# End-node one-hots and the run mask: from one block after the last gathers to single pieces between the groups

## The chip, the cores and the metric

The kernel runs on one core of one Trainium2 chip. The time is device microseconds (us) of one execution. The engines are TensorE (PE, with its weight loads as PEld), VectorE (DVE), ScalarE (ACT), GpSimd (POOL, which here issues the gathers) and SyncE (SP, which issues most other transfers).

## The reference, cut to what matters

Two graph layers run over 12,500 nodes with 256 features and 200,000 edges. The edges come sorted by `dst`.

```python
h = relu(layernorm(x))
x = x + segment_sum(edge_weight * (h @ W)[dst], src)          # first layer
h = relu(layernorm(x))
q, k, v = h @ Wq.T + bq, h @ Wk.T + bk, h @ Wv.T + bv         # 8 heads of 32
sim = sum_d(q[dst] * k[src]) / sqrt(32)                       # per edge and head
p = exp(sim - segment_max(sim, dst)[dst])
attn = p / segment_sum(p, dst)[dst]
x = x + segment_sum(attn * v[src], dst) @ Wo.T + bo           # second layer
```

All is in float32.

## The kernel before, in words

The first layer (`layer0`) sorts the edges by `src` on the chip, gathers rows, sums them by matmuls, and writes the tables Q and KV that the second layer reads. In its course `prep_a`, `prep_c` and `prep_s` turn the edge lists into columns, once for each of four blocks `b` of up to 128 groups. `prep_c` leaves the source ids in `ci0` to `ci3`, and `prep_s` leaves negated places of the end nodes in `nsl0` to `nsl3`. Both are tiles of 128 partitions by 512 elements, in which a group has four columns. `prep_s` also writes to memory, for each group, its first and its last end node (table `PD`).

The second layer (`layer1`) takes the sorted edges in 391 groups of 512, each as four columns of 128 edges. One group passes these steps:

- `load_l1` (three steps ahead): SP loads the 80 rows of Q from the group's first end node on; POOL gathers the KV rows of the 512 edges by four indirect transfers (line 974) that read their ids from `ci`.
- `onehot_t` and `similarity`: ACT makes the transposed one-hots, PE spreads Q to the edges (line 1007), DVE multiplies with K (line 1008) and sums by head (line 1009).
- `softmax_steps`, for eight groups together: DVE scans the maxima of runs of equal end nodes (lines 1030 and 1034), ACT takes the exponential.
- 11 steps later (`LAG`): DVE weighs V (`weigh`, line 1073), ACT makes the one-hots from `nsl` (`onehot`, line 991), PE sums by end node (`aggregate`, line 1085), and the sums go to the table AG.
- Beside these, finished blocks of AG are divided, multiplied by Wo, added to x and stored (lines 836 to 883).

A gathered group lies in one of 15 buffers named `kvt`; a buffer comes free when `weigh` has read it.

An end node can span two or more groups. So the first and last end node of each group are kept apart: 2 x 391 = 782 partial rows (table `PR`), with their maxima in `pm`. `merge_steps` joins them after the groups. It splits the 782 into 7 blocks, one of 14 and six of 128. For each block `k` it needs `S[:, k]` (which rows of the block have the same end node), `C[:, k]` (which rows have the node of the last row of the block before), a count `cnt` of equal rows ahead (only the first of equal rows is stored, the others go to spare rows), the ids `nid` and `idx`, and the mask `mk` of runs for two scans over the 782 maxima.

The function `loads` (step 388 of the loop) brings `PD` in twice: spread over all partitions as `pdr` (line 1183) and as columns `pdc` (lines 1184 and 1185). The function `same` (step 389) then makes `nid`, `C`, `S`, `cnt`, `idx` and `mk` in one go, on DVE (lines 1196 to 1213). The large tiles of the merge are taken from the `kvt` buffers (`big`). Then come `load_rows` (390), `own_rows` (391, gathers of x on POOL, line 1246), `factors` (395, the scans and the exponential), and for each block `total`, `ends_norm`, `ends_turn`, `ends_mult`, `ends_add` and `ends_put`, until step 408.

In both layers the order of work on each engine is the order in which the code is written (a manual schedule). `layer1` runs its steps `t` in order, and a table `todo` hangs further functions at a place 0, 1 or 2 of a step: 0 is between `weigh` of group t - 11 and `similarity` of group t, 1 is after `similarity`, 2 is after `aggregate`. Each engine works its own queue in that order and waits for the others by semaphores.

Of the kernel before, what the change touches and what calls it, by code (L numbers as in the profile page):

```python
# [77 lines left out]
class Gnn:  # L78
# [90 lines left out]
    def prep_c(self, b):  # L169
        nc, cp, wp = self.nc, self.kp, self.wp  # L170
        ng = min(P, NG - b * P)
        si, di, ei = self.raw
        df = self.k0.tile([P, G], F32, name=f"df{b}")
        nc.vector.tensor_copy(df, di)
        self.df[b] = df
        gb = cp.tile([P, 7], F32, name=f"gb{b}")
        nc.vector.tensor_copy(gb[:, 1:2], df[:, 0:1])
        nc.vector.tensor_copy(gb[:, 2:3], df[:, G - 1:G])
        nc.vector.tensor_scalar(gb[:, 3:4], df[:, 0:1], 1.0, None, op0=ALU.add)
        for j, c, o in ((4, PACE * (1 + 1e-5), -OL - 1), (5, PACE * (1 - 1e-5), OU)):  # L180
            v = gb[:, j:j + 1]
            nc.vector.tensor_scalar(v, self.pcol, c, c * (b * P + o), op0=ALU.mult, op1=ALU.add)
            nc.vector.tensor_scalar(v, v, 0.0, None, op0=ALU.max)
            nc.vector.tensor_scalar(v, v, v, None, op0=ALU.mult)
        nc.vector.tensor_scalar(gb[:, 0:1], df[:, 0:1], gb[:, 4:5], float(N - P), op0=ALU.max, op1=ALU.min)
        nc.vector.tensor_scalar(gb[:, 6:7], df[:, 0:1], gb[:, 4:5], gb[:, 5:6], op0=ALU.max, op1=ALU.min)
        gi = cp.tile([P, 7], I32, name=f"gi{b}")
        nc.vector.tensor_copy(gi, gb)
        self.gb[b], self.gi[b] = gb, gi
        sf = wp.tile([P, G], F32, name="sf", bufs=1)  # L190
        nc.vector.tensor_copy(sf, si)
        ci = self.csi[b] = cp.tile([P, P, W], I32, name=f"ci{b}")
        if b < NPT:
            self.cols(sf, ng, [ci])
            return
        sh = wp.tile([P, G], I16, name="sh", bufs=1)
        nc.vector.tensor_copy(sh, si)
        nc.sync.dma_start(self.SR[:ng], sh[:ng])
        l0 = self.l0r = self.k0.tile([P, G], F32, name="l0r")
        nc.vector.tensor_scalar(l0, df, gb[:, 0:1], None, op0=ALU.subtract)  # L200
        self.csf, self.cl0, self.cew = [self.k0.tile([P, P, W], F32, name=f"c{k}") for k in range(3)]
        self.cols(sf, ng, [self.csf, ci])
        self.cols(l0, ng, [self.cl0])
        self.cols(ei, ng, [self.cew])
# [698 lines left out]
    def prep_s(self, b):  # L903
# [24 lines left out]
        nc.vector.tensor_tensor(t, t, sl, op=ALU.max)  # L928
        nc.vector.scalar_tensor_tensor(sl, sl, float(QW + 1), isl, op0=ALU.subtract, op1=ALU.mult)
        nc.vector.tensor_sub(sl, sl, t)  # L930
        self.nsl[b] = self.kp.tile([P, P, W], F32, name=f"nsl{b}")
        self.cols(sl, ng, [self.nsl[b]])
        mk = wp.tile([P, G + 4], F32, name="mk", bufs=1)
        nc.vector.tensor_tensor(t, pf, df, op=ALU.not_equal)
# [2 lines left out]
        nc.vector.memset(mk[:, G:], NEG)  # L937
        nc.sync.dma_start(self.MK[b * P:b * P + ng], mk[:ng])
        nc.sync.dma_start(self.PD[b * 2 * P:(b + 1) * 2 * P].rearrange("(p c) -> p c", c=2), gb[:, 1:3])
        nc.vector.tensor_tensor(t, pf, df, op=ALU.is_gt)  # L940
        nc.vector.tensor_tensor(bad, bad, t, op=ALU.max)
        late = wp.tile([P, 2], F32, name="late")
# [215 lines left out]
    def merge_steps(self):  # L1158
# [7 lines left out]
        def big(n, *shape):  # L1166
            t = wp.tile([P, W * 2 * D], F32, name="kvt", bufs=LAG + PRE + 1)[:, :n]
            if shape:
                t = t.rearrange("p (k d) -> p k d", k=shape[0])
            return t  # L1170

        def size(k):
            return P if k else R0

        def rows(k):
            return slice(R0 + (k - 1) * P, R0 + k * P) if k else slice(0, R0)

        def loads():
            b = big(2 * KB * P)
            pdr, S = b[:, :KB * P], b[:, KB * P:].rearrange("p (k e) -> p k e", k=KB)  # L1180
            pdc = wp.tile([P, KB], F32, name="pdc", bufs=1)
            nc.vector.memset(pdc, -1.0)
            nc.sync.dma_start(pdr, bass.AP(tensor=pd.tensor, offset=pd.offset, ap=[[0, P], [1, KB * P]]))
            nc.sync.dma_start(pdc[:R0, 0:1], pd[:R0][:, None])
            nc.sync.dma_start(pdc[:, 1:, None], bass.AP(tensor=pd.tensor, offset=pd.offset + R0,
                                                        ap=[[1, P], [P, KB - 1], [1, 1]]))
            T.update(pdr=pdr, S=S, pdc=pdc)

        def same():
            pdr, S, pdc = T["pdr"], T["S"], T["pdc"]  # L1190
            cnt = wp.tile([P, KB], F32, name="cntm", bufs=1)
            tr = wp.tile([P, KB], F32, name="trm", bufs=1)
            scr = wp.tile([P, P], F32, name="scrm", bufs=1)
            T["idx"] = wp.tile([P, KB], I32, name="idxm", bufs=1)
            T["nid"] = wp.tile([P, KB], I32, name="nidm", bufs=1)
            nc.vector.tensor_scalar(T["nid"], pdc, 0.0, None, op0=ALU.max)
            T["C"] = big(KB * P, KB)
            for k in range(KB):
                r, m = size(k), pdr[:, rows(k)]
                if k:  # L1200
                    nc.vector.tensor_scalar(T["C"][:, k], m, pdc[:, k - 1:k], self.ident[:, size(k - 1) - 1:size(k - 1)],
                                            op0=ALU.is_equal, op1=ALU.mult)
                nc.vector.tensor_scalar(S[:, k, :r], m, pdc[:, k:k + 1], None, op0=ALU.is_equal)
                nc.vector.scalar_tensor_tensor(scr[:, :r], S[:, k, :r], 1.0, self.lower[:, :r], op0=ALU.mult, op1=ALU.mult,
                                               accum_out=cnt[:, k:k + 1])
            nc.vector.tensor_scalar(tr, cnt, 0.0, self.trash, op0=ALU.is_gt, op1=ALU.mult)
            nc.vector.tensor_tensor(T["idx"], tr, pdc, op=ALU.max)
            b = big(2 * NR + 2)
            mk, f = b[:H, :NR + 1], b[:H, NR + 2:]
            nc.vector.memset(mk[:, 0:1], NEG)  # L1210
            nc.vector.memset(mk[:, NR:], NEG)
            nc.vector.tensor_tensor(mk[:, 1:NR], pdr[:H, 1:NR], pdr[:H, :NR - 1], op=ALU.not_equal)
            nc.vector.tensor_scalar(mk[:, 1:NR], mk[:, 1:NR], NEG, None, op0=ALU.mult)
            T.update(mk=mk, f=f)

        def load_rows():
# [33 lines left out]
        def space(n, w):  # L1250
            T[n] = big(KB * w, KB)

        def total(k):
            r, rt, fc = size(k), T["rt"], T["fc"]
            sc = wp.tile([P, D + H], F32, name="scm", bufs=2)
            nc.vector.tensor_tensor(sc[:r, :D].rearrange("p (h d) -> p h d", h=H),
                                    rt[:r, k, :D].rearrange("p (h d) -> p h d", h=H),
                                    fc[:r, k, :, None].to_broadcast([r, H, DH]), op=ALU.mult)
            nc.vector.tensor_mul(sc[:r, D:], rt[:r, k, D:], fc[:r, k])
            pg = tp.tile([P, G], F32, name="ps", bufs=1)[:, :D + H]  # L1260
            nc.tensor.matmul(pg[:r], T["S"][:r, k, :r], sc[:r], start=True, stop=(k == 0))
            if k:
                q = size(k - 1)
                nc.tensor.matmul(pg[:r], T["C"][:q, k, :r], T["ms"][:q, k - 1], start=False, stop=True)
            nc.scalar.copy(T["ms"][:r, k], pg[:r])

        def ends_norm(k):
# [15 lines left out]
        def ends_put(k):  # L1283
# [3 lines left out]
                in_=T["o"][:r, k], in_offset=None, bounds_check=N - 1, oob_is_err=False)  # L1287

        t = NG + LAG
        steps = [((NG - 3, 0), loads), ((NG - 2, 0), same), ((NG - 1, 0), load_rows), ((NG, 1), own_rows),  # L1290
                 ((NG + 1, 0), lambda: space("ms", D + H)), ((NG + 2, 0), lambda: space("o", D)),
                 ((NG + 4, 0), factors), ((NG + 4, 2), factor_cols), ((NG + 4, 2), lambda: space("an", D)),
                 ((NG + 5, 0), lambda: space("at", D)), ((t + 1, 0), load_rest)]
        for k in range(KB):
            i = NG + 5 + k if k < KB - 1 else t + 2
            steps += [((i, 0), lambda k=k: total(k)), ((i + 1, 0), lambda k=k: ends_norm(k)),
                      ((i + 1, 1), lambda k=k: ends_turn(k)), ((i + 2, 2), lambda k=k: ends_mult(k)),
                      ((i + 3, 0), lambda k=k: ends_add(k)), ((i + 3, 1) if k < KB - 1 else (END, 2), lambda k=k: ends_put(k))]
# [302 lines left out]
    def run(self, hook=lambda k, n: None):  # L1601
# [3 lines left out]
        with ExitStack() as es:  # L1605
# [12 lines left out]
            self.MT = self.dp.tile([N + P, H], F32, name="MT")  # L1618
            self.SS = self.dp.tile([E, H], F32, name="SS")
            self.AG = self.dp.tile([N + P, D + H], F32, name="AG")  # L1620
            self.fl = cp.tile([P, NBLK, 2], F32, name="fl")
            self.hx, self.hv, self.ho, self.hp, self.ha, self.hs, self.ss = {}, {}, {}, {}, {}, 0, 0
            self.pm = cp.tile([H, NBT * NB * 2], F32, name="pm")
# [50 lines left out]
```

## Time and profile before

| | us |
|---|---|
| Median of 3 runs (lowest to highest) | 5429.85 (5414.27 to 5447.61) |
| The profiled execution | 5451.51 |
| its span, first to last instruction | 5449.7 |
| busy: PE / DVE / POOL / ACT | 3826.2 / 3410.1 / 2979.3 / 2200.9 |
| first and last head sum (line 1009) of the second layer, from the span's start | 2644.3 and 5360.9 |

The page of a profile gives the busy time of each engine, the span in 40 slices, the transfers, and groups of equal instructions. The timeline lists the instructions of a stretch in order of time: start, duration, engine, source line, what is written from what, and in brackets the idle time of the engine before it with what ended that. "remote" stands there where no instruction of the program is seen to end the wait. The list of waits sums such idle time by waiting and released line: us in total, times, longest.

### The profile page before, as it was taken

How to read it: one execution, taken by the hardware profiler on the slowest of the kernel's cores; microseconds unless marked ns; L12 is line 12 of the kernel's file. 1: busy time of each engine (PE TensorE's matmuls, PEld its weight loads, DVE VectorE, ACT ScalarE, POOL GpSimd, SP SyncE). 2: the span in 40 equal slices, each digit the busy share in tenths (PEclk: the TensorE clock that was granted, in tenths of full speed). 3: DMA queues.
4: the chain of work that ended last, by engine and by line, in shares of the span. 5: the costliest groups of instructions: out<-in, count | busy, mean ns of one | idle time of the engine just before them, and what ended most of it. 6: DMA issues, size and time to landing. Idle time of an engine off the chain costs nothing. (4 is left out here: it accounts for less than half of the span.)

```text
span 5449.7 us, 61879 instructions
## 1 busy us (share of the span) xinstructions
PE 3826.2 (70%) x14078; PEld 2524.0 (46%) x14078; DVE 3410.1 (63%) x7226; ACT 2200.9 (40%) x6200; POOL 2979.3 (55%) x3096
## 2 busy tenths in 40 slices
PE   4656677656666678778477777777777777677776
PEld 3433344334433344444355555555555555455554
DVE  7877776566666355555255655666666666666665
ACT  5643343223322122222144444444554455454553
POOL 3546655555556566665455555555555555555551
PEclk8877888778878799999677778787888888888888
DMA  6435566555555576666566666676777777676673
GB/s 182 106 97 150 145 176 179 167 158 168 166 153 172 162 204 203 204 198 191 166 191 190 197 199 202 199 206 208 215 209 218 210 213 217 199 215 208 209 221 98
DMA packets 627547, 1004.38 MB, mean 184 GB/s; under 512 B 97274, under 2 KB 450359, under 8 KB 627165
## 3 DMA queue, kind: packets, MB, share of 16 engines
q0 software_dynamic: 196224, 596.49, 39.0%
q1 hardware_dynamic: 430941, 403.79, 23.5%
q8 instruction: 119, 1.95, 0.2%
q14 instruction: 263, 2.15, 0.1%
HBM read 788.60 MB, written 224.47 MB: 186 GB/s over the span
## 5 line engine op out<-in xcount | busy, mean ns | idle before, releaser
L974 POOL DMA_INDIRECT kvt<-KV,ci x1564 | 1498.1, 958 | 1267.6 <-DVE pv L1073 641.4
L644 POOL DMA_INDIRECT hg<-HW,dT x1384 | 1311.9, 948 | 920.9 <-issue 367.4
L1007 PE MATMUL pq<-qt,oht 80*128 80x256 f32 x3128 | 894.0, 433 | 395.7 <-issue 140.5
L664 PE MATMUL pg<-hg,ohs 128*128 128x256 f32 x2768 | 919.7, 453 | 139.1 <-issue 87.0
L1008 DVE TENSOR_TENSOR pr<-pq,kvt 128x512 f32<-128x512 f32 x782 | 516.2, 684 | 800.5 <-remote 527.6
L1085 PE MATMUL pg<-pv,oh 128*82 128x264 f32 x3126 | 941.7, 454 | 78.4 <-DVE pv L1073 63.1
L1007 PEld LDWEIGHTS pq<-qt,oht 80*128 80x128 f32 x3128 | 672.2, 219 | 564.9 <-issue 251.9
L664 PEld LDWEIGHTS pg<-hg,ohs 128*128 128x128 f32 x2768 | 544.4, 217 | 499.2 <-issue 361.1
L991 ACT ACTIVATE oh<-iof,nsl 128x82 f32<-128x82 f32 x1564 | 437.0, 350 | 823.7 <-remote 412.5
L1085 PEld LDWEIGHTS pg<-pv,oh 128*82 128x82 f32 x3126 | 554.3, 182 | 372.2 <-issue 150.9
L653 DVE TENSOR_SCALAR ohs<-iop,sT,eT 128x128 f32<-128x128 f32 x1384 | 472.2, 401 | 124.8 <-remote 50.5
L1073 DVE TENSOR_TENSOR pv<-kvt,pp 128x1024 f32<-128x1024 f32 x391 | 471.1, 1205 | 48.0 <-ACT pb L1062 31.0
L1009 DVE TENSOR_REDUCE sim<-pr 128x32 f32<-128x1024 f32 x391 | 477.0, 1220 | 13.4
L982 ACT ACTIVATE oht<-slt,npcol 80x512 f32<-80x512 uint8 x391 | 282.1, 721 | 280.0 <-remote 130.3
L663 PE MATMUL pg<-wn,cs 128*1 128x256 f32 x746 | 254.5, 427 | 184.0 <-ACT wn L685 80.0
L685 ACT COPY wn<-pg 128x256 f32<-128x256 f32 x373 | 137.8, 370 | 407.1 <-PE pg L664 189.1
L467 ACT ACTIVATE sd<-mv,eps 128x1 f32<-128x1 f32 x128 | 37.7, 295 | 584.8 <-DVE sd L472 301.0
L711 PE MATMUL tps<-wkv,ht 128*128 128x512 f32 x512 | 263.1, 640 | 0.0
L983 ACT ACTIVATE oht<-oht 80x512 f32<-80x512 f32 x391 | 246.4, 630 | 12.3
L243 DVE COPY_PREDICATED W<-m,vp 128x512 f32<-128x512 int32 x317 | 228.3, 720 | 20.8 <-ACT vp L231 20.6
L231 ACT COPY vp<-W 128x512 f32<-128x512 f32 x344 | 203.2, 591 | 59.7 <-DVE W L243 42.4
L445 DVE TENSOR_TENSOR xh<-pt,xh 128x256 f32<-128x256 f32 x152 | 63.9, 421 | 249.2 <-PE pt L440 126.5
(304 smaller groups left out, 4553.0 us busy)
## 6 DMA issues: line engine op xcount, KB each, us to landing
KV<-K SPq DMA_DIRECT2D x128, 256.0 KB
AG<-ag SPq DMA_DIRECT2D x391, 82.5 KB
tw<-acc SPq DMA_DIRECT2D x248, 128.0 KB
acc<-ws SPq DMA_DIRECT2D x248, 128.0 KB
qt<-Q SPq DMA_DIRECT2D x391, 80.0 KB
kvt<-KV,ci POOLq DMA_INDIRECT x1564
hg<-HW,dT POOLq DMA_INDIRECT x1384
xh<-acc SPq DMA_DIRECT2D x152, 128.0 KB
```

Source lines behind the costliest of these rows:

```text
L644: nc.gpsimd.indirect_dma_start(out=hg[:, w], out_offset=None, in_=self.HW, in_offset=bass.IndirectOffsetOnAxis(ap=self.part[b][0][:, c:c + ...
L653: self.nc.vector.tensor_scalar(oh[:, w], self.iop, sT[:, c], eT[:, c], op0=ALU.is_equal, op1=ALU.mult)
L664: nc.tensor.matmul(pg, oh[:, w], hg[:, w], start=(w == 0), stop=(w == n - 1))
L711: nc.tensor.matmul(X["kv"], X["ht"][:, k], self.wkv[:, k], start=(k == 0), stop=(k == 1))
L974: nc.gpsimd.indirect_dma_start(out=kv[:, w], out_offset=None, in_=self.KV, in_offset=bass.IndirectOffsetOnAxis(ap=self.csi[b][:, p, w:w + ...
L982: nc.scalar.activation(oht, sl, AF.Abs, bias=self.npcol[:QW])
L991: nc.scalar.activation(oh[:, w], self.iof[:, :MA], AF.Abs, bias=self.nsl[b][:, p, w:w + 1])
L1007: nc.tensor.matmul(pq[:, c], oht[:, 2 * a + c], qt, start=True, stop=True)
L1008: nc.vector.tensor_mul(pr[:, 2 * a:2 * a + 2], pq, kv[:, 2 * a:2 * a + 2, :D])
L1009: nc.vector.tensor_reduce(sim[:, :, i, :], pr.rearrange("p w (h d) -> p w h d", h=H), op=ALU.add, axis=AX.X)
L1073: self.nc.vector.tensor_tensor(pv[:, :, :D].rearrange("p w (h d) -> p w h d", h=H), kv[:, :, D:].rearrange("p w (h d) -> p w h d", h=H), s ...
L1085: nc.tensor.matmul(pg, oh[:r, w], pv[:r, w], start=(w == 0), stop=(w == nw - 1))
```

## The change

- The four tiles `ci0` to `ci3` become one tile `CI`, and `nsl0` to `nsl3` become one tile `NSL`. Both are allocated at the start of `run`.
- `prep_s` makes the mask of runs from what it has at hand (does the group's first edge start a new node; do its first and last node differ) and writes it to a new table `ME`, once for each block.
- `loads` moves from step 388 to step 286, place 1. `pdr` now lies in the first 896 columns of `NSL`, and `S` in the first 896 of `CI`: columns of groups below 224, all of which are behind the loop by then. `C` is no longer a tile: `same` writes it over `pdr` in place.
- `same` becomes a function of one block `k`, and runs at steps 296, 305, ..., 350, place 0. The ids are made by `own_ids` at step 366. The mask is loaded by `load_mask` at step 389.
- Two of the ten `kvt` buffers that the merge took are no longer taken.

```diff
+        me = wp.tile([P, 2], F32, name="me")
+        nc.vector.tensor_tensor(me[:, 0:1], pf[:, 0:1], base, op=ALU.not_equal)
+        nc.vector.tensor_copy(me[:, 1:2], ne)
+        nc.vector.tensor_scalar(me, me, NEG, None, op0=ALU.mult)
+        nc.sync.dma_start(self.ME[b * 2 * P:(b + 1) * 2 * P].rearrange("(p c) -> p c", c=2), me)
...
         def loads():
-            b = big(2 * KB * P)
-            pdr, S = b[:, :KB * P], b[:, KB * P:].rearrange("p (k e) -> p k e", k=KB)
+            pdr = self.NSL.rearrange("p b g w -> p (b g w)")[:, :KB * P]
+            S = self.CI.rearrange("p b g w -> p (b g w)")[:, :KB * P].bitcast(F32).rearrange("p (k e) -> p k e", k=KB)
...
-        def same():
...
-            T["C"] = big(KB * P, KB)
-            for k in range(KB):
...
+            T["C"] = {k: pdr[:, rows(k)] for k in range(1, KB)}
+
+        def same(k):
+            S, pdc, cnt = T["S"], T["pdc"], T["cnt"]
+            r, m = size(k), T["pdr"][:, rows(k)]
+            scr = wp.tile([P, P], F32, name="scrm", bufs=1)
+            nc.vector.tensor_scalar(S[:, k, :r], m, pdc[:, k:k + 1], None, op0=ALU.is_equal)
+            nc.vector.scalar_tensor_tensor(scr[:, :r], S[:, k, :r], 1.0, self.lower[:, :r], op0=ALU.mult, op1=ALU.mult,
+                                           accum_out=cnt[:, k:k + 1])
+            if k:
+                q = size(k - 1)
+                nc.vector.tensor_scalar(m, m, pdc[:, k - 1:k], self.ident[:, q - 1:q], op0=ALU.is_equal, op1=ALU.mult)
+
+        def own_ids():
+            tr = wp.tile([P, KB], F32, name="trm", bufs=1)
+            nc.vector.tensor_scalar(T["nid"], T["pdc"], 0.0, None, op0=ALU.max)
+            nc.vector.tensor_scalar(tr, T["cnt"], 0.0, self.trash, op0=ALU.is_gt, op1=ALU.mult)
+            nc.vector.tensor_tensor(T["idx"], tr, T["pdc"], op=ALU.max)
+
+        def load_mask():
             b = big(2 * NR + 2)
             mk, f = b[:H, :NR + 1], b[:H, NR + 2:]
-            nc.vector.memset(mk[:, 0:1], NEG)
             nc.vector.memset(mk[:, NR:], NEG)
-            nc.vector.tensor_tensor(mk[:, 1:NR], pdr[:H, 1:NR], pdr[:H, :NR - 1], op=ALU.not_equal)
-            nc.vector.tensor_scalar(mk[:, 1:NR], mk[:, 1:NR], NEG, None, op0=ALU.mult)
+            nc.sync.dma_start(mk[:, :NR], bass.AP(tensor=self.ME.tensor, offset=self.ME.offset, ap=[[0, H], [1, NR]]))
...
-        steps = [((NG - 3, 0), loads), ((NG - 2, 0), same), ((NG - 1, 0), load_rows), ((NG, 1), own_rows),
+        steps = [((286, 1), loads), ((366, 0), own_ids), ((NG - 2, 0), load_mask), ((NG - 1, 0), load_rows), ((NG, 1), own_rows),
...
+        steps += [((296 + 9 * k, 0), lambda k=k: same(k)) for k in range(KB)]
```

More of the change, by code (lines that the diff above doesn't have):

```diff
@@ L191, in prep_c @@
         nc.vector.tensor_copy(sf, si)
-        ci = self.csi[b] = cp.tile([P, P, W], I32, name=f"ci{b}")
+        ci = self.csi[b] = self.CI[:, b]
         if b < NPT:
@@ L930, in prep_s @@
         nc.vector.tensor_sub(sl, sl, t)
-        self.nsl[b] = self.kp.tile([P, P, W], F32, name=f"nsl{b}")
+        self.nsl[b] = self.NSL[:, b]
         self.cols(sl, ng, [self.nsl[b]])
@@ L1187, in loads @@
             T.update(pdr=pdr, S=S, pdc=pdc)
-        def same():
[L1190 to L1193, printed above, removed]
+            T["cnt"] = wp.tile([P, KB], F32, name="cntm", bufs=1)
             T["idx"] = wp.tile([P, KB], I32, name="idxm", bufs=1)
             T["nid"] = wp.tile([P, KB], I32, name="nidm", bufs=1)
-            nc.vector.tensor_scalar(T["nid"], pdc, 0.0, None, op0=ALU.max)
-            T["C"] = big(KB * P, KB)
-            for k in range(KB):
[L1199 to L1207, printed above, removed]
@@ L1263, in total @@
                 q = size(k - 1)
-                nc.tensor.matmul(pg[:r], T["C"][:q, k, :r], T["ms"][:q, k - 1], start=False, stop=True)
+                nc.tensor.matmul(pg[:r], T["C"][k][:q], T["ms"][:q, k - 1], start=False, stop=True)
             nc.scalar.copy(T["ms"][:r, k], pg[:r])
@@ L1620, in run @@
             self.AG = self.dp.tile([N + P, D + H], F32, name="AG")
+            self.NSL = cp.tile([P, NBLK, P, W], F32, name="nsl")
+            self.CI = cp.tile([P, NBLK, P, W], I32, name="ci")
+            self.ME = self.dp.tile([NBLK * 2 * P], F32, name="ME")
             self.fl = cp.tile([P, NBLK, 2], F32, name="fl")
```

## The prediction

> **What bounds the kernel.** I read the page first, for size.
>
> ```profile
> span 5449.7 us, 61879 instructions
> ## 1 busy us (share of the span) xinstructions
> PE 3826.2 (70%) x14078; PEld 2524.0 (46%) x14078; DVE 3410.1 (63%) x7226; ACT 2200.9 (40%) x6200; POOL 2979.3 (55%) x3096
> ```
>
> No engine is full. The edit touches the second layer (span 2644 to the end), so next I read DVE's waits over its groups, 2720 to 5340, and POOL's over the whole span:
>
> ```profile
> DVE pr L1008 <- remote: 491.9, 76, 10.4
> DVE pr L1008 <- PE pq L1007: 99.3, 88, 5.3
> DVE o L873 <- remote: 93.0, 14, 9.3
> ```
> ```profile
> POOL kvt L974 <- DVE pv L1073: 641.4, 133, 38.9
> ```
>
> POOL waits for buffers that DVE frees, so the gathers do not set the pace; DVE, PE and ACT do. They run close together, with pauses: 76 + 14 waits of DVE, 584.9 us, 6.5 us each, one per 29 us. One of them in the timeline shows ACT and DVE standing still together, with no instruction seen to release them:
>
> ```profile
> 5320.21 1.12 ACT L991 ACTIVATE oh<-iof,nsl 128x82 f32<-128x82 f32 x4 [9.29 <-remote]
> 5320.27 0.42 DVE L873 TENSOR_TENSOR o<-pq,ox 128x256 f32<-128x256 f32 x1 [7.66 <-remote]
> ```
>
> What these pauses are, the trace does not say. The chain of waits on the page holds only the last 2 us and is of no use here. So I read the timeline where the old `same` stands:
>
> ```profile
> 5343.98 1.21 DVE L1073 TENSOR_TENSOR pv<-kvt,pp 128x1024 f32<-128x1024 f32 x1
> ...
> 5346.30 0.17 DVE L1196 TENSOR_SCALAR nidm<-pdc 128x7 int32<-128x7 f32 x1 [1.11 <-DMA pdc<-PD]
> 5346.38 0.23 DVE L1203 TENSOR_SCALAR kvt<-kvt,pdc 128x14 f32<-128x14 f32 x1
> ...
> 5346.74 0.34 DVE L1201 TENSOR_SCALAR kvt<-kvt,pdc,ident 128x128 f32<-128x128 f32 x1
> 5347.00 0.28 DVE L1203 TENSOR_SCALAR kvt<-kvt,pdc 128x128 f32<-128x128 f32 x1
> 5347.32 0.29 DVE L1204 SCALAR_TENSOR_TENSOR scrm<-kvt,lower 128x128 f32<-128x128 f32 x1
> ...
> 5351.98 0.95 DVE L1212 TENSOR_TENSOR kvt<-kvt 8x781 f32<-8x781 f32 x1
> ...
> 5353.45 0.40 DVE L873 TENSOR_TENSOR o<-pq,ox 128x256 f32<-128x256 f32 x1
> ...
> 5354.68 0.29 PEld L863 LDWEIGHTS pq<-ident,an 128*128 128x128 f32 x2 [8.63 <-DVE an L851]
> ...
> 5355.41 0.37 ACT L864 COPY at<-pq 128x256 f32<-128x256 f32 x1 [9.87 <-PE pq L863]
> ```
>
> DVE leaves the groups at 5345.19 (43.98 + 1.21) and comes back at 5353.45. PE and ACT stand idle in that time and wait for it. POOL has issued its last gather by 5337.3. This block is therefore on the path.
>
> **The change part by part.**
>
> *Taken from step 389.* 5353.45 - 5345.19 = 8.26 us: 1.11 us of waiting for `pdc` and 7.15 us of work. One memset of 0.06 us stays there. Gain **8.2 us**, if nothing else is late. What could be late next? The gathers of groups 389 and 390: their semaphores show landings up to 5341.1, so they are not. The Q rows for 390 were issued at 5337.0. PE's products for group 389 end at 5346.5, about when DVE, after 1.1 us of other work there, would ask for them. The mask's load is one transfer on SP, needed by `factors` at 5376, about 30 us on. The x rows (L1246, from 5363.5) are used at 5398. Steps 390 to 408 keep their order and slide forward as a whole; the two freed `kvt` buffers let `load_rows` and `own_rows` issue two steps sooner, which nobody waits for. A pause could also fall into the freed place; this is a rival below.
>
> *Put between the groups.* By the rows, block 0 is 5346.38 to 5346.74 = 0.36 us, and each of the six others 5346.74 to 5347.53 = 0.79 us (L1201, L1203, L1204 and its 0.08 read of the sum): 0.36 + 6 x 0.79 = 5.1 us. The three small operations of `own_ids` add about 0.4. Together 5.5 us of DVE, in eight steps. Is there room? DVE is busy 284 of the 440 us from 4700 to 5140, where these steps lie, which is 2.4 us idle for each of about 64 steps; but much of it is pauses, and a block placed at a step without one delays `similarity`. In the steps near 5307 DVE waited 0.79 + 0.49 us for PE's products (5308.36, 5309.54), just in the place where a block would go; in the step before, 0. So between 0 and 5.5; I take half, **2.8 us**. If that cover is gone, it is 5.5.
>
> *`loads` at step 286.* The memset is 0.06 us. SP's three issues were 0.35, 0.33 and 0.39 us at 5340.9 to 5342.4. They now stand ahead of the AG store of step 286 and the Q load of group 290, which comes three steps before its use. SP waits for the memset behind `similarity`; the AG store queued next waits for ACT's copy, later in that step. 448 KB more move while the DMA share is 0.69, less while it is 0.35. Between 0 and 1.1 (the three issues); I take 0. The first user, step 296, is ten steps (some 65 us) later; the 1.11 us wait for `pdc` is not moved but gone.
>
> *The mask in `prep_s`.* Three small operations on each of four blocks. Nearest rows: `ne` (L923) 0.15 us, `nidm` 0.17. About 0.4 us a block, 1.7 in all. They stand ahead of a 0.68 us reduction on DVE, at 1203 to 1606, where DVE is not full. The added store (0.35 to 0.43 us on SP, like L939) makes SP wait about 0.4 us more for DVE; the zeroing of AG and the next `tw` load, four groups ahead, queue behind it. Between 0 and 3.4 (4 x 0.85); I take half of DVE's part, **0.8 us**.
>
> *Memory.* The order of the built program shows that L991 and L974 get no new wait from the merged tiles, as the rewritten columns belong to finished groups. The `kvt` buffers keep their addresses. Cost 0.
>
> *Where a rule speaks against it.* In the old place POOL is idle; in the new one it issues gathers in most steps. The Trainium skill, page "SBUF — State Buffer", section "Who interferes with whom", says that a DVE `tensor_scalar` that enters a two-port mode shares an exclusive port pair with GpSimd, and that the later one waits out the whole instruction of the other. The new blocks have 13 `tensor_scalar` from SBUF to SBUF (7 for S, 6 for C), and L974 takes 0.95 us. By the rule the worst is 13 x 0.95 = 12.3 us. The row of the trace that stands where the blocks will stand, between gathers, is the `tensor_scalar` of the division:
>
> ```profile
> L849 DVE TENSOR_SCALAR os<-oa x87: 153/164/410, 3050.3 to 5337.1; 128x8 f32<-128x8 f32 x87
> ```
>
> Minimum, median and maximum in ns: the longest of 87 is 0.25 us over the median, and none waited out a gather. Mean 193 against a median of 164 gives 13 x 0.03 = 0.4 us. The row decides; I count it within the 2.8. The rule's 12.3 stays as the upper end and as a rival. The other direction, a gather held up by a DVE block (at most 13 x 0.34 = 4.4 us of POOL), falls on an engine that waits 641 us anyway.
>
> **Sum.** -8.2 + 2.8 + 0 + 0.8 = **-4.6 us**. The profiled execution took 5451.51 us (span 5449.7 and 1.8 around it): 5446.9 for it. It stands 21.7 above the median of the runs, 5429.85, and I give the forecast at that level: **5425 us**.
>
> **Rivals.**
>
> 1. *A pause takes the freed place.* DVE's 8 us standstill lies where none of the pauses is seen (none after 5320), though they come one per 29 us. If the old block hid one, or one now falls into steps 389 and 390, 6.5 us come back: -4.6 + 6.5 = +1.9, 5432 us. For: PE and ACT stood still in the same way. Against: PE's load falls after step 390, and no pause appears there.
> 2. *Slower: the port.* Place: the 13 `tensor_scalar` at steps 296 to 350. Price: up to 0.95 us each. -4.6 + 12.3 = +7.7, about 5438 us. It decides from 4.6 / 13 = 0.35 us of waiting each. For: the rule, and L849's longest, 0.41. Against: L849's median.
> 3. *It does not do what it says:* the end is held by something else that is no faster, such as the AG stores or the last `PR` load (issued 5420.16), and the 8 us turn into waiting there. Then +2.8 + 0.8 = +3.6, 5433 us. Against: L1240 waits for stores that themselves follow the steps in order.
> 4. *The pauses fall differently throughout.* The same program spread over 33 us in three runs, several times the edit. A shift of 54 us or more, either way, would need some eight pauses gained or lost; nothing in the views asks for it.
>
> **How the numbers follow.** Forecast 0.50; pause 0.25; port 0.11; held elsewhere 0.06; other pauses 0.08. The forecast's own bounds: -8.2 (all hidden) to +0.7 (5.5 + 3.4), so 5422 to 5431. The likeliest is 5425. With rivals 1 to 3 the median may lie from 5422 to 5438, and the median of a few runs moves by some 15 us besides (5414 to 5448 before): 5404 to 5450. One per cent, 54 us, is about what a measurement of this kernel can tell from no change; the first four cases lie within it, and the last is split: faster 0.04, same 0.92, slower 0.04.
>
> **What would show it.** Right: in the new profile DVE goes from `weigh` at step 389 to `similarity` without the 8 us, PE's idle time before its transpose there falls from 8.6 to about 2, and the distance from step 388's head sum (5342.8) to step 389's falls from 13.1 to about 5; from 5360.9 to the end stays near 89 us. The blocks show 0.8 us each, `tensor_scalar` near 0.28 and 0.34. Wrong in parts: a "remote" gap in steps 389 to 391 (rival 1); `tensor_scalar` of 0.6 us and more between gathers (rival 2); a stretch from step 390 to the end that is 8 us longer (rival 3). The forecast as a whole is wrong if the groups before step 286 have changed their pace.

## The result and the profile after

The changed kernel took 5430.99 us (median, 5409.06 to 5463.95), the kernel before, timed beside it, 5432.79 us (5407.21 to 5456.76). The ratio is 1.0002, with a 95% interval from 0.9986 to 1.0019: between 8 us faster and 10 us slower, no difference that the total can show. Whether the sum of -4.6 us is right has to be read from the places where its parts lie.

The page of the changed kernel has the same mix of work as before. Its span is 36.9 us shorter than that of the profile of before:

```profile
span 5412.8 us, 61893 instructions
## 1 busy us (share of the span) xinstructions
PE 3821.9 (71%) x14078; PEld 2523.8 (47%) x14078; DVE 3412.0 (63%) x7235; ACT 2207.1 (41%) x6200; POOL 2989.4 (55%) x3096
```

Nine more instructions on DVE, 1.9 us more busy time. To split the 36.9 us I use the starts of the head sum (`sim<-pr`, the last operation of `similarity`): 12.4 us lie ahead of the first one and 18.0 between the first and that of step 388, where the edit takes nothing away. Only 6.6 lie from step 388 to the end. So most of the 36.9 us lies where the edit saves nothing; executions of one program differ as much (5409.06 to 5463.95 for the changed kernel). The edit is seen in the timeline at step 389 of the changed kernel (start, us, engine, line, operation, tiles; in brackets the idle time before and what ended it):

```profile
5313.56 1.21 DVE L1078 TENSOR_TENSOR pv<-kvt,pp 128x1024 f32<-128x1024 f32 x1
5314.69 0.42 DVE L873 TENSOR_TENSOR o<-pq,ox 128x256 f32<-128x256 f32 x1
5314.71 0.06 DVE L1218 MEMSET kvt<- 8x1 f32 x1
...
5315.81 1.28 DVE L1013 TENSOR_TENSOR pr<-pq,kvt 128x512 f32<-128x512 f32 x2
5315.94 0.20 PEld L863 LDWEIGHTS pq<-ident,an 128*128 128x128 f32 x2 [0.31 <-DVE an L851]
...
5316.41 0.37 ACT L864 COPY at<-pq 128x256 f32<-128x256 f32 x1 [1.30 <-PE pq L863]
5317.12 1.22 DVE L1014 TENSOR_REDUCE sim<-pr 128x32 f32<-128x1024 f32 x1
...
5325.03 0.42 DVE L873 TENSOR_TENSOR o<-pq,ox 128x256 f32<-128x256 f32 x1 [1.98 <-remote]
```

`weigh` (L1078) is followed by the division and `similarity` at once; only the memset of the mask's last column is left. PE's weight load waited 0.31 us instead of 8.63, ACT's copy 1.30 instead of 9.87. The last line is what the sum didn't have: a wait that was not there before, in the step after 390, and ended by no instruction that is seen.

The distances between head sums, in us, for all profiles in which the tail's code is that of one of the two kernels, or nearly so. The last column is the median of the kernel before on the same chip: the runs fell on several, and two profiles are best compared within one of them.

| kernel | blocks at | 388 to 389 | 389 to 390 | 390 to end | 388 to end | before there |
|---|---|---|---|---|---|---|
| before | 389 | 13.02 | 5.00 | 88.9 | 106.9 | 5432.8 |
| after | groups | 4.70 | 3.58 | 92.1 | 100.3 | 5432.8 |
| e1 | 389, nine times | 52.68 | 5.76 | 88.4 | 146.9 | 5490.0 |
| e3 | 389 | 11.81 | 5.52 | 88.6 | 105.9 | 5490.0 |
| e2 | groups | 5.62 | 4.49 | 90.7 | 100.9 | 5490.0 |
| e4 | groups | 4.70 | 5.09 | 91.8 | 101.6 | 5490.0 |
| e11 (before) | 389 | 13.18 | 5.28 | 89.3 | 107.7 | 5495.4 |
| e10 (changed) | groups | 4.70 | 4.37 | 93.8 | 102.8 | 5495.4 |
| e12 | groups | 4.70 | 9.43 | 91.3 | 105.4 | 5495.4 |
| e9 | groups | 4.70 | 3.58 | 92.5 | 100.8 | 5495.4 |
| e5 | 389 | 10.25 | 6.49 | 93.1 | 109.9 | 4279.1 |
| e8 | groups | 4.70 | 3.58 | 92.3 | 100.6 | 4279.1 |
| e6 | groups | 4.81 | 4.16 | 94.2 | 103.2 | 4279.1 |
| e7 | groups | 4.70 | 3.58 | 95.5 | 103.8 | 4279.1 |

### The profile page after: what moved, and what is told of

It reads as the page before. It is cut to its first block, busy times and chain, and to the rows that moved or that the text cites. A ratio compares the mean times of both kernels' runs of the same rounds, so it can differ in the third digit from the quotient of the medians.

```text
span 5412.8 us, 61893 instructions
## 1 busy us (share of the span) xinstructions
PE 3821.9 (71%) x14078; PEld 2523.8 (47%) x14078; DVE 3412.0 (63%) x7235; ACT 2207.1 (41%) x6200; POOL 2989.4 (55%) x3096
## 2 busy tenths in 40 slices
DMA packets 628140, 1004.42 MB, mean 186 GB/s; under 512 B 97858, under 2 KB 450943, under 8 KB 627757
## 5 line engine op out<-in xcount | busy, mean ns | idle before, releaser
L664 PE MATMUL pg<-hg,ohs 128*128 128x256 f32 x2768 | 906.1, 447 | 129.1 <-issue 93.1
L1078 DVE TENSOR_TENSOR pv<-kvt,pp 128x1024 f32<-128x1024 f32 x391 | 471.4, 1206 | 47.8 <-ACT pb L1067 32.8
L988 ACT ACTIVATE oht<-oht 80x512 f32<-80x512 f32 x391 | 246.9, 632 | 12.4
```

The costliest lines, as they stand in the source:

```text
L664: nc.tensor.matmul(pg, oh[:, w], hg[:, w], start=(w == 0), stop=(w == n - 1))
L1078: self.nc.vector.tensor_tensor(pv[:, :, :D].rearrange("p w (h d) -> p w h d", h=H), kv[:, :, D:].rearrange("p w (h d) -> p w h d", h=H), s ...
```

## Experiments

Theory: the block at step 389 was on the path one to one, some of what it frees comes back soon after, blocks in the groups cost little, the mask in `prep_s` costs something. Rivals: a pause takes the freed place; blocks beside gathers are slow or delay the groups; the end is held elsewhere.

### 1. The old block nine times as long

In the kernel before:

```
-            for k in range(KB):
+            for k in list(range(KB)) * 9:
```

> The kernel before, with the seven S/cnt/C blocks of step 389 made nine times over (the same values each time): 8 x 5.1 = 41 us more of VectorE at that one place. Theory (the old block lay wholly on the path): 41 us longer, ratio about 1.0075, all of it between the head sums of steps 388 and 389 (13.0 us before, about 54 then), and the stretch from step 390 to the end unchanged near 89 us. Rival (the block's time is partly taken back by work or pauses that would have come anyway): less than 30 us.

5534.37 us, ratio 1.0068 [1.0043, 1.0094], which is 37 us (24 to 52; the medians are 44 apart). In its profile 388 to 389 took 52.68 us, 39.7 more than in before, and 390 to the end 88.4. So the block is paid in full, and nothing after it gives it back. That speaks against rival 3: the end follows this block.

### 2. A block in every step

In the changed kernel, ahead of each `similarity`, three operations of a block's kind on tiles that nobody reads:

```
+            if t < NG:
+                self.filler()
+    def filler(self):
+        ...
+        nc.vector.tensor_scalar(s, self.iof, self.pcol, None, op0=ALU.is_equal)
+        nc.vector.scalar_tensor_tensor(s, s, 1.0, self.lower, op0=ALU.mult, op1=ALU.mult, accum_out=n[:, 0:1])
+        nc.vector.tensor_scalar(s, self.iof, self.pcol, self.ident[:, P - 1:P], op0=ALU.is_equal, op1=ALU.mult)
```

> The kernel after, with one further block of about 0.8 us (equality, masked product with sum, equality times a column; written to scratch) ahead of similarity in each of the 391 steps: 0.8 x 391 = 310 us more of VectorE in the groups. If a block in the groups costs its whole time, the kernel is 310 us longer (ratio 1.057); if it is half hidden, as the prediction took, 155 us (1.029); if it is hidden, under 30 us. Port rival: the tensor_scalar rows that meet a running gather are 0.6 us and longer; else 0.27 and 0.34.

5492.30 us, ratio 1.0004 [0.9982, 1.0025]: 2 us above the kernel before (-10 to 14); the changed kernel itself was not timed on this chip. The groups of lines of its profile say what was added (count, then busy us and mean ns, then idle before):

```profile
L1171 DVE TENSOR_SCALAR scrm<-iof,pcol,ident 128x128 f32<-128x128 f32 x391 | 140.0, 358 | 14.3
L1170 DVE SCALAR_TENSOR_TENSOR scrm<-scrm,lower 128x128 f32<-128x128 f32 x391 | 123.7, 316 | 13.5
L1169 DVE TENSOR_SCALAR scrm<-iof,pcol 128x128 f32<-128x128 f32 x391 | 110.6, 283 | 0.0
```

374 us by these lines. They overlap with each other and with the work beside them, so DVE's busy time grew by 326 us over the page of the changed kernel (3412.0 to 3738.1), 0.83 a step, and there is nothing to see in the total. Where it went is in DVE's waits from 2720 to 5330 (us in total, times, longest), first of the changed kernel, then of this one:

```profile
DVE pr L1013 <- remote: 471.5, 76, 10.2
DVE o L873 <- remote: 111.3, 18, 9.4
DVE pr L1013 <- PE pq L1012: 81.9, 84, 4.2
DVE pr L1013 <- issue: 78.1, 106, 9.0
```
```profile
DVE pr L1013 <- remote: 324.8, 58, 7.6
DVE o L873 <- remote: 67.8, 10, 7.9
DVE pr L1013 <- PE pq L1012: 41.5, 33, 3.8
...
DVE pr L1013 <- issue: 17.3, 34, 4.1
```

These four waits fall from 742.8 to 451.4 us, 291 less: DVE works in the time in which it had waited. So the pauses are not DVE's own. By the semaphore records of the trace of before, of the 799 us for which `pr` waits 691 end within 25 ns of a signal of PE. It is PE's products that come late; why PE is late the trace doesn't say.

### 3. A block in every third step of the kernel before

The same filler, `if t < NG and t % 3 == 0`, 131 times.

> The kernel before, with the same further block in every third step: 131 x 0.8 = 105 us more of VectorE. Whole cost 105 us (ratio 1.019), half hidden 52 us (1.010), hidden under 10 us. Its end is that of the kernel before, so the distance from the head sum of step 388 to the end should again be near 107 us.

5498.07 us, ratio 1.0016 [1.0002, 1.0029]: +9 us (1 to 16) for 111 us more of DVE's busy time (3410.1 to 3520.8), 0.07 us a block. For seven blocks that is 0.5 us, and by experiment 2 less.

### 4. The mask's operations forty times

In the changed kernel, `for _ in range(40):` ahead of the three operations in `prep_s`.

> The kernel after, with the three small mask operations of the first layer made 40 times in each of the four blocks: 39 x 0.35 to 0.4 us x 4 = 55 to 62 us more of VectorE, in four lumps of 14 to 16 us. Whole cost 55 to 62 us (ratio 1.010 to 1.011), half hidden 30 us. The second layer unchanged: from the head sum of step 388 to the end near 100 us.

5568.14 us, ratio 1.0121 [1.0081, 1.0161]: +66 us over before (44 to 88; the medians are 78 apart). Its groups of lines:

```profile
L944 DVE TENSOR_SCALAR me<-me 128x2 f32<-128x2 f32 x160 | 28.0, 175 | 5.5
L942 DVE TENSOR_TENSOR me<-pf,gb 128x1 f32<-128x1 f32 x160 | 25.6, 160 | 5.6
L943 DVE COPY me<-ne 128x1 f32<-128x1 f32 x160 | 23.5, 147 | 0.0
```

77.1 us of busy time where the changed kernel has 1.9. The same DVE that hides 326 us in the groups hides little or none of these here. But four lumps of 19 us can be paid where four single pieces of 0.42 us are hidden, so the single mask has to be read too. First of before, then of the changed kernel, the last operation ahead of the mask's place that both have, and the matmul that waits for DVE behind it:

```profile
1200.02 0.69 DVE L930 TENSOR_TENSOR sl<-sl,t 128x512 f32<-128x512 f32 x1
1204.85 0.46 PE L433 MATMUL pt<-h 128*128 128x128 f32 x2 [1.25 <-DVE xh L445]
```
```profile
1197.22 0.69 DVE L930 TENSOR_TENSOR sl<-sl,t 128x512 f32<-128x512 f32 x1
1202.38 0.46 PE L433 MATMUL pt<-h 128*128 128x128 f32 x2 [1.60 <-DVE xh L445]
```

From start to start it is 4.83 us in before and 5.16 in the changed kernel, and DVE's last small operation of `prep_s` (`fl`) is 0.33 us later, counted from the same L930, in each of the four blocks. So PE does wait for the mask, 0.33 of its 0.42 us a block, about 1.3 us in all; whether all of it reaches the end of the layer is not shown.

### 5. The blocks back at step 389, all else as changed

```
-        steps = [((286, 1), loads), ((366, 0), own_ids), ((NG - 2, 0), load_mask), ...
+        steps = [((286, 1), loads), ((NG - 2, 0), load_mask), ((NG - 2, 0), lambda: [same(k) for k in range(KB)]),
+                 ((NG - 2, 0), own_ids), ...
-        steps += [((296 + 9 * k, 0), lambda k=k: same(k)) for k in range(KB)]
```

> The changed kernel with the seven blocks and the three operations of own_ids moved back to step 389; the early loads, the memory of dead columns and the mask from prep_s stay. By the theory (the block stands on the path 1:1, and some 2 to 3 us of what is freed come back after step 390 because PE and ACT have no products in stock): the distance of the head sums of steps 388 and 389 grows from 4.7 to about 10 us (5.5 of work), the stretch from step 390 to the end falls from about 92 to about 89, and 388 to the end is about 103 to 106 against 100 to 101.6 with the change. By the rival (the freed time came from the vanished wait for pdc and the mask alone, and the blocks were hidden behind PE): 388 to 389 stays under 6.

This ran on a chip where the kernel before takes 4279.12 us; one run of this kernel took 4287.81, which alone says nothing of the total. 388 to 389 was 10.25 us, 5.55 more than without the blocks, the 5.5 of the prediction. DVE's timeline shows them one after the other with no wait, from the end of `weigh` to the `o` of the next division:

```profile
4177.31 1.21 DVE L1078 TENSOR_TENSOR pv<-kvt,pp 128x1024 f32<-128x1024 f32 x1
4178.44 0.23 DVE L1202 TENSOR_SCALAR ci<-nsl,pdc 128x14 f32<-128x14 f32 x1
...
4183.29 0.34 DVE L1207 TENSOR_SCALAR nsl<-nsl,pdc,ident 128x128 f32<-128x128 f32 x1
4183.55 0.16 DVE L1211 TENSOR_SCALAR nidm<-pdc 128x7 int32<-128x7 f32 x1
...
4183.98 0.42 DVE L873 TENSOR_TENSOR o<-pq,ox 128x256 f32<-128x256 f32 x1
```

From step 390 to the end it was not 89 but 93.1. Put against the timeline of before, instruction by instruction, DVE keeps the same times within 0.4 us for 29 us after step 390 and is then 3.3 us late at one `o` (idle 3.46 us ahead of it, 0.56 in before). There PE ran at half clock for 14 us (granted 0.57 from 4211 to 4227); in before only 3.4 us of that stretch were at half clock. The same wait, 3.6 us long, is in e6, e8, e10 and e12 and, 2.3 long, in e2 and e7, each with 10 to 14 us at half clock there. So it belongs to neither place of the blocks. It is in no profile of the kernel before, though, nor in after, e4 and e9; whether another part of the edit draws it there is open. With the blocks back, nothing is late just after step 390, as was expected.

### 6 and 7. One more matmul, one more Relu in every step

In the changed kernel: `pq[:, 1]` made twice; `oht` passed through Relu once more (the values don't change).

> The changed kernel with one more matmul in each of the 391 steps (the second product of pq made twice, 0.436 us each, 170 us in all; the result is the same). The earlier runs hid 0.8 to 1.0 us of DVE work per step. Theory P (PE sets the pace of the groups, and DVE waits for it): the total grows by about 170 us, ratio near 1.03, and DVE's idle time in the groups grows by about the same. Theory S (pauses or the gathers set the pace and every engine has slack): the total grows by less than 40 us.

> The changed kernel with one more Relu over oht on ACT in each of the 391 steps (0.63 us each, 247 us in all; the result is the same). Theory P (PE alone sets the pace): ACT's addition is hidden as DVE's was, ratio under 1.01. Rival (ACT stands on the path, since PE waits for oht): the total grows by 100 to 250 us, ratio 1.02 to 1.045.

On the same chip: 4280.22 us, ratio 1.0008 [0.9992, 1.0024], with PE busy 102 us longer than in e5 (3450.9 to 3553.2); 4298.88 us, ratio 1.0047 [1.0033, 1.0062], +20 us for 246 us more of ACT. Neither engine alone set the pace there. But this chip isn't in the same regime. Busy time in the groups (us of PE, PEld, DVE, ACT and POOL with counts, then granted clock, DMA share, GB/s), first of the changed kernel of the first timing, then of e7:

```profile
2720.00:5310.00 2590.00, 1946.40 (x7378) 1398.52 (x7377) 1640.57 (x2164) 1297.64 (x3614) 1444.61 (x1503) 0.82 0.70 208
```
```profile
2200.00:4160.00 1960.00, 1696.08 (x7366) 1263.44 (x7365) 1636.97 (x2163) 1514.45 (x3982) 1452.71 (x1515) 0.93 0.90 277
```

The same groups take three quarters of the time: the clock is 0.93 instead of 0.82, the DMA share 0.90 instead of 0.70, and not one "remote" wait is listed for DVE over this stretch. With the pauses gone the transfers are the fullest resource. So experiments 6 and 7 say nothing of what makes PE late on the first chips; that stays open. Nor was the changed kernel as it stands timed on this chip, or a block added to every step there, where DVE is busy 0.84 of the time.

### 8. The mask in the groups

If DVE work in the groups is free and that in `prep_s` is not, the mask belongs in the groups. In `loads` two more transfers bring the end nodes shifted by one, and at step 293:

```
+            nc.vector.tensor_tensor(me, T["pdc"], me, op=ALU.not_equal)
+            nc.vector.tensor_scalar(me, me, NEG, None, op0=ALU.mult)
+            nc.sync.dma_start(self.ME[:R0][:, None], me[:R0, 0:1])
+            nc.sync.dma_start(bass.AP(tensor=self.ME.tensor, ..., ap=[[1, P], [P, KB - 1], [1, 1]]), me[:, 1:, None])
```

> The changed kernel with the mask made in the second layer instead of in prep_s: a second copy of the end nodes shifted by one is loaded at step 286 into dead columns, two operations on 128x7 at step 293 make the mask, two stores put it to ME; the three operations and the store in each prep_s block are gone. By the theory (DVE work in the groups costs nothing, that in prep_s its whole time) it is 1.7 us faster than the changed kernel: the second layer starts 1.7 us sooner after the first layer's own pauses are set aside, and the tail from step 388 is the same, 100 to 102 us. Against the kernel before: 5 to 8 us, ratio about 0.999, which the total can hardly show. By the rival (the mask was hidden in prep_s as well) there is no difference anywhere.

4289.06 us, ratio 1.0019 [1.0008, 1.0029]: slower than before by 8 us. A miss. The changed kernel was not timed beside it; the nearest is e6, with a ratio of 1.0008 [0.9992, 1.0024], so how much of the 8 us comes from the mask's move is not sharply known. The timeline shows one place:

```profile
3672.47 0.34 SPq L1213 DMA_DIRECT2D ME<-ci  x1
3672.86 0.39 SPq L1214 DMA_DIRECT2D ME<-ci  x1
3673.56 0.36 SPq L836 DMA_DIRECT2D oa<-AG  x1
...
3685.45 0.17 DVE L849 TENSOR_SCALAR os<-oa 128x8 f32<-128x8 f32 x1 [9.06 <-DMA oa<-AG]
```

The two stores write one number per packet, 4 bytes (the page counts 98905 packets under 512 bytes, against 97858 in e5). The load of `oa` is issued right behind them, and DVE waits 9.06 us for it; on this chip no wait for `oa` in the groups of e5 was longer than 4.8. The step took 13.84 us; the median step of this profile took 5.1. By the packet records the 4-byte packets were through by 3677, and three packets of AG rows begun at 3676.4 to 3676.8 took 2.7 to 6.0 us; no other packet of that queue in this profile took over 2.5. So the wait follows from the transfers and not from DVE's two operations. It is seen once, in one profile.

### 9 to 12. Yardsticks, more loads, and the mask in an idle place

e10 is the changed kernel, e11 the kernel before. e12 has the two loads of `pdc` nine times over, into dead columns:

```
+            for j in range(8):
+                nc.sync.dma_start(more[:R0, j * KB:j * KB + 1], pd[:R0][:, None])
+                nc.sync.dma_start(more[:, j * KB + 1:(j + 1) * KB, None], ...)
```

e9 drops mask and `ME` from `prep_s`, loads the end nodes into the mask's tile at step 389 and adds at step 394, where DVE stood idle for 1.94 us:

```
+            nc.vector.tensor_tensor(f[:, 1:], mk[:, 1:NR], mk[:, :NR - 1], op=ALU.not_equal)
+            nc.vector.tensor_scalar(mk[:, 1:NR], f[:, 1:], NEG, None, op0=ALU.mult)
```

> The changed kernel once more, as a yardstick on the chip of this call. In the first timing it was 1.0002 [0.9986, 1.0019] times the kernel before. By the sum corrected with the runs so far (tail 6 us shorter, mask 1.7 us longer, blocks hidden) it is 4 to 5 us faster, ratio 0.999. On a chip of the second kind (granted clock near 0.92, no pauses of DVE, DMA share near 0.9 in the groups), where the loads of step 286 seem to hold up the load of oa, it may be 0 to 3 us slower instead: ratio 0.999 to 1.001. Tail from step 388: 100 to 102 us.

> The kernel before, for its profile on the same chip as the changed one. Theory (the block of step 389 is on the path whatever the chip): 388 to 389 is 12 to 13 us, 388 to the end 105 to 108 us, against 4.7 and 100 to 104 with the change. Steps 285 to 295, where the changed kernel has its three loads: if the loads cost nothing, the same as with the change within 2 us; if they cost, 3 to 6 us shorter.

> The changed kernel with the two loads of pdc (782 packets of 4 bytes) made nine times at step 286, the eight more into dead columns that nobody reads. Theory L (packets of 4 bytes stand in the queue ahead of the loads that the groups wait for; moving the mask into the groups had put as many to ME and DVE then waited 9.06 us for oa): steps 285 to 295 grow by 25 us or more, and DVE waits there for a DMA. Rival (the loads are hidden in the groups, and the 9.06 us came of the stores of 4 bytes alone): under 6 us, of which SP's 16 issues of 0.35 us are the only part that can show.

> The changed kernel with the mask made in neither place: load_mask brings the end nodes themselves into the mask's tile, and two operations (0.95 us each) make the mask at step 394, where DVE stood idle 1.94 us in the changed kernel; the three operations and the store in each prep_s block are gone. By the theory it saves 1.7 us in the first layer and costs nothing at step 394 (tail from 388 still 100 to 102 us): 1.7 us faster than the changed kernel, too little for the total to show, so it is read from the tail's length. By the rival (what fills an idle place of DVE comes back at the next wait) the tail is 1.5 to 2 us longer and the gain is nothing.

With before at 5495.43 us: e10 5491.10, ratio 0.9998 [0.9980, 1.0016]; e12 5497.93, 1.0003 [0.9988, 1.0018]; e9 5491.68, 0.9996 [0.9978, 1.0014]; e11 gave one time, 5497.33. From step 388 to the end e11 took 107.7 and e10 102.8: 4.9 us gained, 6.6 in the first pair. Steps 285 to 295, with the early loads in e10 and without in e11, took 69.3 and 66.2 us here, but 65.9 and 70.6 in the first pair: no cost that stands out of the pauses.

In e12 those ten steps took 78.7 us, but 76.2 in e9, which has no loads added; pauses blur it. DVE waited for a load once in that stretch, 7.75 us, but also 6.92 us at step 230, where nothing had been added, so the extra pairs need not be the reason. And a pause fell into step 390:

```profile
4732.72 0.17 DVE L849 TENSOR_SCALAR os<-oa 128x8 f32<-128x8 f32 x1 [7.75 <-DMA oa<-AG]
```
```profile
5420.81 1.29 DVE L1013 TENSOR_TENSOR pr<-pq,kvt 128x512 f32<-128x512 f32 x2 [5.76 <-remote]
```

The total of e12 is 7 us above e10, inside the noise of both; 25 us and more did not come, and neither bound of the expectation (under 6, over 25) is met clearly. Whether loads of 4 bytes cost the groups something on the fast chip, where the transfers are fuller, wasn't tried.

In e9 the mask (0.95 and 0.55 us) fits into the idle place, and the wait behind it shrinks by as much, 1.94 to 0.48 us:

```profile
5407.53 1.21 DVE L1073 TENSOR_TENSOR pv<-kvt,pp 128x1024 f32<-128x1024 f32 x1
5408.66 0.95 DVE L1219 TENSOR_TENSOR kvt<-kvt 8x781 f32<-8x781 f32 x1
5409.65 0.55 DVE L1220 TENSOR_SCALAR kvt<-kvt 8x781 f32<-8x781 f32 x1
5410.68 1.22 DVE L1073 TENSOR_TENSOR pv<-kvt,pp 128x1024 f32<-128x1024 f32 x1 [0.48 <-ACT pb L1062]
```

The tail is 100.8 us, as short as with the mask from `prep_s`. In `prep_s` the four distances of experiment 4 are those of before again. By its places e9 should be the best version by about 1.3 us; its total doesn't show that.

## Why the prediction was right, point by point

**Taken from step 389: -8.2.** The freed time was right: 388 to 389 fell by 8.32 us (13.02 to 4.70), and experiment 1 shows that the block had been paid in full. Another 1.4 us were gained up to step 390 (5.00 to 3.58), which the prediction didn't have, and 3.2 were lost behind it. In both places DVE's waits are for PE: in before 1.07 and 0.17 us in step 390, in after the two waits at `o` below. PE's clock in the two stretches, from head sum 388 to 390 and over the next 12 us (busy us of PE, PEld, DVE, ACT and POOL with counts, then granted clock, DMA share, GB/s), first of before, then of after:

```profile
5342.85:5360.87 18.02, 9.79 (x40) 7.21 (x39) 15.18 (x47) 5.31 (x17) 0.00 (x0) 0.81 0.26 70
5360.87:5372.87 12.00, 9.00 (x44) 6.07 (x43) 10.90 (x17) 6.83 (x22) 7.24 (x7) 1.00 0.61 175
```
```profile
5312.42:5320.70 8.28, 8.28 (x40) 6.39 (x39) 8.14 (x13) 5.33 (x17) 4.41 (x5) 1.00 0.43 123
5320.70:5332.70 12.00, 8.60 (x35) 5.76 (x33) 8.73 (x12) 4.98 (x18) 2.22 (x3) 0.86 0.49 154
```

In before a stretch of half clock (1.0 and 0.5 are all that is granted) ends 3.1 us ahead of step 390's head sum; in after none lies between 388 and 390. Behind 390 it is the other way round. In after PE's signal for the product that `o` waits for comes 4.30 us after that head sum; in e8, the same code in this place, 1.85. PE gives no signal at all from 2.53 us ahead of it to 2.86 us behind, though its records show matmuls begun at 5319.72, 5321.51 and 5322.37. To DVE this looks like the pauses in the groups; it waits 1.98 us, and no instruction is seen to end the wait. A stretch of half clock follows, from 6.8 to 10.2 us, and the next `o` waits 1.45 us for PE. So -8.3 - 1.4 + 3.2 = -6.5, against 8.2: the term was sized too large by 1.7 us in this pair and by 3.3 in the pair e10 and e11, where the tail is 4.9 us shorter.

**Put between the groups: 2.8.** Too large: on these chips experiments 2 and 3 allow 0 to 0.5 us for seven blocks. Taking half between the bounds had no ground in a row; DVE's waits for PE, from which the cover could be read, were already shown.

**`loads` at step 286: 0.** Held on the first kind of chip, where before and after differ in both directions.

**The mask in `prep_s`: 0.8.** Too small, for the same reason, halving: 1.3 us by the distances in the four blocks, and experiment 4 allows the whole 1.7.

**Sum.** -6.5 + 0.3 + 0 + 1.3 = -4.9 us in the first pair and -4.9 + 0.3 + 0 + 1.3 = -3.3 in the second, beside the -4.6 forecast. Three errors cancel, which is luck: the sum came out for a partly wrong reason. Both timed pairs, 1.0002 and 0.9998, hold it and also hold zero, so the total confirms no more than that the change is small.

**Rival 1, a pause in the freed place.** It came, smaller than its 6.5 us. Its sign, a "remote" gap of DVE in steps 389 to 391, is there in five of the six profiles of the new tail on the first kind of chip: 1.98 us in after, 1.35 in e10, 2.13 in e9, 1.41 in e4, and 5.76 in e12, whose tail of 105.4 us has lost most of the gain. It is in none of the old tail (before, e1, e3, e11) and none on the fast chip (e5 to e8). The prediction counted the pause as 6.5 us or nothing; it took a part in most cases. Whether such a pause would have come in the old code too, unseen while DVE stood in the block and PE waited, is not shown. A rival reading is that PE and ACT work ahead during the old block and the new code lacks that stock; it fits badly, as at the first `o` behind 390 DVE is not late at all in e6, e7 and e8, which lack the stock too.

**Rival 2, the port.** Not seen for these operations. The blocks in the changed kernel (minimum, median, maximum in ns):

```profile
L1202 DVE TENSOR_SCALAR ci<-nsl,pdc x7: 228/281/383, 4687.0 to 5057.0; 128x128 f32<-128x128 f32 x6, 128x14 f32<-128x14 f32 x1
L1207 DVE TENSOR_SCALAR nsl<-nsl,pdc,ident x6: 337/338/347, 4754.9 to 5057.6; 128x128 f32<-128x128 f32 x6
```

The longest of the 13 is 0.10 us over its median; none waited out a gather of 0.95 us, though all six of L1207 ran beside one. In experiment 2, 391 pairs average 283 and 358 ns and the longest are 0.51 and 0.56 us; 230 and 370 of them ran beside a gather. Whether they enter a two-port mode at all, the trace does not say.

**Rival 3, the end held elsewhere.** The tail got shorter in every pair; not so.

**Rival 4, pauses throughout.** They do move single profiles by tens of us, but no median moved.

## What to carry to other kernels

Before giving a cost to work put on an engine, look at whose result that engine waits for: DVE waited for PE in the groups and took 326 us of extra work for nothing, while in a stage where PE waits for DVE most of 0.42 us was passed on. When a stop is taken away, read the steps behind it in several profiles, with the granted clock beside them: here PE's pauses and stretches of half clock fell elsewhere than before, and 2 to 3 us came back. A moved step brings its transfers along: DVE waited 9 us for a load behind two stores of 4-byte packets, where the arithmetic cost nothing.

## What the runs showed of the hardware

The kernel before took 5433 to 5495 us on three chips and 4279 on a fourth. On the first three PE was granted 0.82 to 0.83 of its clock in the mean, and in the profile of before DVE had 80 waits at `pr`, of 6.6 us on average, in which nothing was seen to release it. On the fourth the clock was 0.92, and in the groups of e6 and e7 no such wait was listed. These pauses are therefore not of the program alone.

The pauses and the half clock go together. In before, between the first head sum and that of step 388, PE stands still by its records 94 times for over 3 us, in 0.19 of the time. Of the 119 stretches of half clock that begin there, 72 begin inside such a stop, 70 of them more than 1.5 us after its start. So there the half clock follows the stop and doesn't begin it; what stops PE stays open.

In e9 a `tensor_scalar` on 8 x 781 numbers took 0.55 us where the `tensor_tensor` of the same size took 0.95.
